# Two edits in a two-layer transformer kernel: where an attention pair's step ends, and where a convolution's last tap is written

## The chip, the cores and the metric

The kernel runs on one core of one Trainium2 chip. The core has four compute engines with a queue each: TensorE (PE, with its weight loads shown as PEld), VectorE (DVE), ScalarE (ACT) and GpSimd (POOL); a fifth, SyncE (SP), issues the DMAs here. Every queue is worked off in order, and an instruction waits on semaphores for what it needs. The metric is the device time of one execution in microseconds, the median of several.

## The reference, cut to what matters

Two layers work on x of 16 sequences, 512 tokens and 256 channels, in float32. In each layer a modulation made from a small conditioning vector scales and shifts a layer norm, and gates what is added back.

- Layer 0 projects to q, k and v, runs a causal convolution of four taps over the tokens of each channel, then Silu; these feed a recurrence of "fast weights" over chunks of 16 tokens, which goes through the tokens in order. A low-rank feed-forward part follows.
- Layer 1 is attention with 16 heads of 16 channels. A token sees the 64 latest tokens and, besides, the first four tokens of its sequence (the global keys). A feed-forward part that mixes each token with the one before it (channel mix) follows.

```
y = lax.conv_general_dilated(xT, w[:, None, :], ..., padding=[(KSZ - 1, 0)], feature_group_count=x.shape[-1])
...
q = l2norm(jax.nn.silu(short_conv(hidden_states @ Wq.T, cq)).reshape(b, l, H, HD))
...
mask = local | g_row & causal | g_col & causal
att = jnp.where(mask, att, jnp.finfo(att.dtype).min)
att = jax.nn.softmax(att, axis=-1)
```

## The kernel before, in words

The work is cut into 16 units: half of the sequences (8) times a block of 64 tokens. A unit u goes through five streams: `prepare` (layer norm, projections and convolutions), `chain` (the recurrence, on DVE, POOL and ACT), `mlp` (end of layer 0's first part and the low-rank feed-forward), `attend` (window attention) and `mix` (channel mix). Each stream is a Python generator, and what lies between two `yield`s is a step. A timetable gives every step a due time in units (`prepare` 12 steps from u - 1.7 to u - 0.7, `chain` 28 steps from u to u + 2, `attend` 24 steps, 19 of them from u + 3.05 to u + 3.95), and the steps of all units are written in the order of these times. So moving a `yield` moves instructions ahead of, or behind, the steps of other streams. From the written order the framework makes the order of each engine's queue; it lets a later instruction go first where an earlier one isn't ready by its plan, and it places buffers and semaphores. The table functions Silu, Gelu and Tanh are issued as bursts (`run`, L220 to L235), the first of a burst waiting for all that the burst needs, so that ACT's table is loaded once for each burst and once back (L224, L234).

Buffers are rings: eight PSUM banks are one for the fast weights (`fw`), three under the tag "bank" (`bank`), four under "abank" (`abank`). SBUF tiles of 2 KB a partition are rings by stream: three for stream a, six for stream c.

Convolution (`prepare`, L434 to L474), for q, k and v (n) and each half of the channels (k2), one step each: PE makes the projection in a bank pp (L441); ACT copies it behind three old columns into xp (L454) and scales the bank by the last weight plus one (L457); DVE adds the other three taps into the same bank (L459). A third step runs the burst of both halves' Silus from the banks to the SBUF tiles y (L465, timed at L224), and SP spills y to DRAM in two pieces each (L468).

Attention works on four pairs of sequences in a unit (r). `find_maxima` (L877) makes the scores sc and their maxima mx (L888), which POOL splits in parts (L215, L217). `weigh` (L904) does the rest of a pair: two filler matmuls (`hold`, L197), a transposition of the maxima (pmx, L908, and mxT, L910), then the scores st again with keys on the partitions, less the maxima (mm, L872), into four banks of "abank"; the mask by a matmul (`add_mask`, L869); the exponentials pT (L926); where the block isn't one of the first two ("far"), also scores tg over the global keys with two fillers, and their exponentials pg (L938); then py (weights times values) and pz (the sums), into two banks of "abank"; then 1/pz as rs (L976, L977) and the product yT (L981). After two pairs, pproj (L1003) projects them, and the gated sum is added to x (up_c, L387, and x, L389).

Other names that the prediction uses: pq and pk are attention's projections (L800, L812); up_a and up_b are the gated sums of layer 0; hp is channel mix's normed input (L367), sg its gate (L1085); e_k and e_v are the recurrence's exponentials (L541), pd_o, pd_i and pd_kv its outer products on POOL (L533), tok its token copies (L596); pgate (L480) is a projection at the end of `prepare`.

Of the kernel before, what the change touches and what calls it, by code (L numbers as in the profile page):

```python
# [12 lines left out]
AF = mybir.ActivationFunctionType  # L13
# [4 lines left out]
P = 128  # L18
# [3 lines left out]
TB = 64  # L22
HB = 8
# [72 lines left out]
def adaln_blocks(ctx: ExitStack, tc: tile.TileContext, a: dict, out: bass.AP):  # L96
    nc = tc.nc
    mul, add, sub = ALU.mult, ALU.add, ALU.subtract
# [12 lines left out]
    def bank(name):  # L111
        return ps.tile([P, 512], F32, tag="bank", name=name)

    def abank(name):
        return ps_a.tile([P, 512], F32, tag="abank", name=name)
# [4 lines left out]
    def t2k(stream, name, shape=None):  # L120
        return work.tile(shape or [P, 512], F32, tag=f"t2k_{stream}", name=name, bufs=RING[stream])
# [23 lines left out]
    conv_w = []  # L145
# [74 lines left out]
    def run(burst, after):  # L220

        with tc.high_priority():
            for k, args in enumerate(burst):
                ins = nc.scalar.activation(*args[0], **args[1])  # L224
                for dep in after if k == 0 else ():
                    tc.add_manual_dep(
                        ins.ins,
                        dep.ins.name,
                        mybir.DependencyInfo(mybir.DependencyClass.Sync, mybir.DependencyReason.DATA),
                        reason="one load of the table",  # L230
                    )
                if k > 0:
                    tc.keep_in_program_order(ins)
            back = nc.scalar.preload_act_table_set("natural_log_exp_and_others")  # L234
            tc.keep_in_program_order(back)  # L235
# [86 lines left out]
    def spill(name, shape):  # L322
        spilled[name] = dram.tile(shape, F32, tag=name, name=name)
        return spilled[name]
# [7 lines left out]
    def hidden(stream, name, cols=TB):  # L332
        t = work.tile([P, 2 * HB * (TB + 1)], F32, tag=f"hT_{stream}", name=name, bufs=1)
        return t[:, : 2 * HB * cols].rearrange("p (k b t) -> p k b t", k=2, b=HB)
# [59 lines left out]
    def place(u):  # L394

        return u % NH, u // NH
# [7 lines left out]
    def load_x(u, name, tag, bufs):  # L404
        x = stage.tile([P, NR, C], F32, tag=tag, name=name, bufs=bufs)
        for e in range(2):
            nc.sync.dma_start(x[e * TB : (e + 1) * TB], rows(a["x"], u, e))
        return x

    def prepare(u):  # L410
        half, tb = place(u)
        b0 = half * HB
        bs = slice(b0, b0 + HB)
        for pc in range(NPC):
            for n in "qkvo":
                spill(f"{n}{u}_{pc}", [HB, H, D, PT])
            spill(f"lr{u}_{pc}", [HB, H, 2, PT])
        x = load_x(u, f"xa{u}", "xa", 1)
        hT = hidden("a", f"hTa{u}")
        yield from norm_T(x, 0, 0, b0, f"a{u}", hT)  # L420
        hf = [hT[:, k].rearrange("p b t -> p (b t)") for k in range(2)]

        pp = bank(f"plr{u}")
        for k in range(2):
            nc.tensor.matmul(pp[: 2 * H, :], lhsT=w_lr[:, k, :], rhs=hf[k], start=k == 0, stop=k == 1)
        lrT = t2k("a", f"lrT{u}", [P, HB, TB])[: 2 * H]
        nc.scalar.copy(lrT.rearrange("p b t -> p (b t)"), pp[: 2 * H, :])
        for pc in range(NPC):
            nc.sync.dma_start(
                spilled[f"lr{u}_{pc}"].rearrange("b h j t -> (h j) b t"),  # L430
                lrT[:, :, pc * PT : (pc + 1) * PT],
            )

        for n in range(3):  # L434
            ys, convs = [], []
            for k2 in range(2):
                tg = tails[:, 2 * n + k2, bs, :]
                tag = f"{u}_{n}_{k2}"
                pp = bank(f"pp{tag}")
                for k in range(2):  # L440
                    nc.tensor.matmul(  # L441
                        pp,
                        lhsT=w_qkv[n][:, k, k2 * P : (k2 + 1) * P],
                        rhs=hf[k],
                        start=k == 0,
                        stop=k == 1,
                    )
                ppb = pp.rearrange("p (b t) -> p b t", b=HB)
                xp = work.tile([P, HB, TB + 3], F32, tag="xp", name=f"xp{tag}", bufs=2)
                if tb == 0:  # L450
                    nc.gpsimd.memset(xp[:, :, 0:3], 0.0)
                else:
                    nc.gpsimd.tensor_copy(xp[:, :, 0:3], tg)
                nc.scalar.copy(xp[:, :, 3:], ppb)  # L454
                if tb < T // TB - 1:
                    nc.gpsimd.tensor_copy(tg, xp[:, :, TB:])
                nc.scalar.activation(ppb, ppb, AF.Copy, scale=conv_w[n][:, k2, 3:4])  # L457
                for j in range(3):
                    ins = nc.vector.scalar_tensor_tensor(  # L459
                        ppb, xp[:, :, j : j + TB], conv_w[n][:, k2, j : j + 1], ppb, mul, add  # L460
                    )
                ys.append((t2k("a", f"y{tag}", [P, HB, TB]), ppb))
                convs.append(ins)
                yield
            run([((y, ppb, AF.Silu), {}) for y, ppb in ys], convs)  # L465
            for k2, (y, _) in enumerate(ys):
                for pc in range(NPC):
                    nc.sync.dma_start(  # L468
                        spilled[f"{'qkv'[n]}{u}_{pc}"][:, k2 * H // 2 : (k2 + 1) * H // 2].rearrange(
                            "b h d t -> (h d) b t"  # L470
                        ),
                        y[:, :, pc * PT : (pc + 1) * PT],
                    )
            yield  # L474

        gT = spill(f"gT{u}", [P, 2, HB * TB])
        for k2 in range(2):
            pp = bank(f"pgate{u}_{k2}")
            for k in range(2):
                nc.tensor.matmul(  # L480
                    pp, lhsT=w_g[:, k, k2 * P : (k2 + 1) * P], rhs=hf[k], start=k == 0, stop=k == 1
                )
            gsb = t2k("a", f"gsb{u}_{k2}")
            nc.scalar.copy(gsb, pp)
            nc.sync.dma_start(gT[:, k2], gsb)
# [283 lines left out]
    def window_attention(i, x):  # L769
# [4 lines left out]
        far, last = tb > 1, tb == T // TB - 1  # L774
# [96 lines left out]
        def mm(dst, lhsT, rhs, start=False):  # L871
            nc.tensor.matmul(dst, lhsT=lhsT, rhs=rhs, start=start, stop=False, skip_group_check=True)  # L872
# [31 lines left out]
        def weigh(r, outs):  # L904
            tag, q = f"{i}_{r}", queries(r)
# [11 lines left out]
            for s, k2, e in slots:  # L917
                for j in range(4):
                    rows = slice(32 * j, 32 * (j + 1))
                    mm(st[j][:, s * P : (s + 1) * P], sel[rows, s : s + 1].to_broadcast([32, P]), mxT[rows])  # L920
            yield
            pT = []
            for j in range(4):
                add_mask(st[j], False)
                pT.append(t2k("c", f"pT{tag}_{j}"))
                nc.scalar.activation(pT[j], st[j], AF.Exp)  # L926
            py, pz = abank(f"py{tag}"), abank(f"pz{tag}")
            if far:

                rg = slice(32 * r, 32 * (r + 1))  # L930
                tg = bank(f"tg{tag}")
                for s, k2, e in slots:
                    mm(tg[rg, e * P : (e + 1) * P], kglob[:, b0 + 2 * r + e, 16 * k2 : 16 * k2 + 32], q(k2, e), s == 0)
                for e in range(2):
                    mm(tg[rg, e * P : (e + 1) * P], selg[:, e], mxT)
                hold(tg[:, 2 * P :], 2)
                pg = work.tile([P, 2 * P], F32, tag="pg", name=f"pg{tag}", bufs=1)
                nc.scalar.activation(pg[rg], tg[rg, : 2 * P], AF.Exp)  # L938
                for s, k2, e in slots:
                    for j in range(4):  # L940
                        cols = slice(k2 * P + 32 * j, k2 * P + 32 * (j + 1))
                        mm(
                            py[32 * j : 32 * (j + 1), s * P : (s + 1) * P],
                            vglob[half][rg, e, cols],
                            pg[rg, e * P : (e + 1) * P],
                            s == 0,
                        )
                for k2 in range(2):
                    for j in range(4):
                        n = 4 * k2 + j  # L950
                        mm(
                            pz[32 * j : 32 * (j + 1), k2 * 2 * P : (k2 + 1) * 2 * P],
                            ones_g[rg, n : n + 1].to_broadcast([32, 32]),
                            pg[rg],
                            k2 == 0,
                        )
# [236 lines left out]
```

## Time and profile before

| | |
|---|---|
| three runs, us | 3237.48, 3243.3 and 3245.96; median 3243.3 |
| profiled execution, us | 3245.84, its span 3244.0 |
| granted TensorE clock, mean | 0.823 |
| PE, DVE, ACT, POOL busy | 75%, 73%, 54%, 52% |
| the convolutions' taps, L459 | 288 of some 750 ns, 215.2 us |
| pT exponentials, L926 | 256 of 619 ns, 133.6 us |
| y Silus, L224 | 96 of 594 ns, 52.1 us |

Busy time of an engine is the union of its instructions; PE's is no measure of how well the array is used. "Idle before" an instruction is the time that its engine stood still ahead of it, with what released it. The chain of waits is followed back from the last instruction, each step to what released it, or to the instruction before it on its engine.

### The profile page before, as it was taken

How to read it: one execution, taken by the hardware profiler on the slowest of the kernel's cores; microseconds unless marked ns; L12 is line 12 of the kernel's file. 1: busy time of each engine (PE TensorE's matmuls, PEld its weight loads, DVE VectorE, ACT ScalarE, POOL GpSimd, SP SyncE). 2: the span in 40 equal slices, each digit the busy share in tenths (PEclk: the TensorE clock that was granted, in tenths of full speed). 3: DMA queues.
4: the chain of work that ended last, by engine and by line, in shares of the span. 5: the costliest groups of instructions: out<-in, count | busy, mean ns of one | idle time of the engine just before them, and what ended most of it. 6: DMA issues, size and time to landing. Idle time of an engine off the chain costs nothing.

```text
span 3244.0 us, 47232 instructions
## 1 busy us (share of the span) xinstructions
PE 2445.9 (75%) x17232; PEld 1472.7 (45%) x17232; DVE 2372.1 (73%) x4513; ACT 1762.4 (54%) x3738; POOL 1677.1 (52%) x1575
## 2 busy tenths in 40 slices
PE   3541156778787778988888888988888888889996
PEld 2110124444444445555455555554545555556564
DVE  1678787878868878878888888878878877873221
ACT  1652354555664656665665656565665545454543
POOL 0245555556656655655646565655556556553112
PEclk8775577878877887988889797989889787879898
DMA  5331112131403223130413122231404121112010
GB/s 150 75 69 20 46 34 70 31 73 39 97 17 77 62 57 76 48 85 21 103 30 94 45 68 65 51 83 34 99 14 105 28 70 37 57 39 59 17 28 27
DMA packets 439307, 186.46 MB, mean 57 GB/s; under 512 B 323937, under 2 KB 413090, under 8 KB 439074
## 3 DMA queue, kind: packets, MB, share of 16 engines
q1 hardware_dynamic: 439074, 183.44, 23.4%
q8 instruction: 135, 2.21, 0.3%
q14 instruction: 98, 0.80, 0.1%
HBM read 116.66 MB, written 66.72 MB: 57 GB/s over the span
## 4 chain that ended last, share of the span: by engine, by line
DVE 35%; POOL 22%; PE 21%; ACT 10%; issue 8%; DMA 3%; SPq 1%; POOLq 0%; DVEq 0%; ACTq 0%
POOL pd_o L533 6%; POOL pd_i L533 5%; DVE pd_kv L630 3%; DVE sc_v L526 3%; DVE pp L459 3%; DVE sv L527 3%; DVE mx L888 2%; DVE do L635 2%; PE st L872 2%; DVE di L635 2%; POOL pd_kv L533 2%; DVE scs L527 2%; PE pQ L742 1%; PE ph L735 1%; PE py L872 1%
## 5 line engine op out<-in xcount | busy, mean ns | idle before, releaser
L533 POOL TENSOR_TENSOR pd_o<-e_k,dt_v 128x1024 f32<-128x1024 f32 x128 | 299.4, 2346 | 242.0 <-DVE e_k L548 242.0
L533 POOL TENSOR_TENSOR pd_i<-e_v,dt_k 128x1024 f32<-128x1024 f32 x128 | 297.3, 2358 | 30.7 <-DVE e_v L548 30.7
L660 POOL TENSOR_TENSOR pd_kv<-hid,pd_kv 128x1024 f32<-128x1024 f32 x64 | 150.5, 2351 | 175.3 <-DVE fw L631 149.3
L872 PE MATMUL st<-qs,keys 32*128 32x128 f32 x2048 | 203.4, 321 | 46.2 <-DVE yT L981 23.3
L635 DVE TENSOR_REDUCE di<-pd_i 128x64 f32<-128x1024 f32 x128 | 155.6, 1216 | 108.6 <-POOL pd_i L533 108.6
L872 PEld LDWEIGHTS st<-qs,keys 32*128 32x128 f32 x2048 | 168.6, 211 | 122.0 <-DVE yT L981 34.3
L872 PE MATMUL sc<-keys,qs 32*128 32x128 f32 x2048 | 167.3, 327 | 74.1 <-DVE yT L981 47.9
L635 DVE TENSOR_REDUCE do<-pd_o 128x64 f32<-128x1024 f32 x126 | 152.9, 1215 | 91.2 <-POOL pd_o L533 91.2
L707 PE MATMUL pwo<-w_WoT,oT 128*128 128x256 f32 x256 | 107.0, 579 | 136.7 <-POOL oT L700 135.9
L872 PEld LDWEIGHTS sc<-keys,qs 32*128 32x128 f32 x2048 | 133.3, 215 | 141.0 <-DVE yT L981 51.2
L888 DVE TENSOR_REDUCE mx<-sc 128x4 f32<-128x512 f32 x256 | 168.0, 682 | 18.5 <-PE sc L869 18.3
L526 DVE TENSOR_TENSOR sc_k<-tok,fw 128x1024 f32<-128x1024 f32 x128 | 155.7, 1216 | 13.8 <-ACT tok L596 12.1
L533 POOL TENSOR_TENSOR pd_kv<-hid,dt_v 128x1024 f32<-128x1024 f32 x64 | 150.5, 2352 | 25.7 <-DVE hid L622 22.7
L630 DVE TENSOR_TENSOR_SCAN pd_kv<-within,pd_kv 128x1024 f32<-128x1024 bf16 x64 | 156.4, 2443 | 0.7
L526 DVE TENSOR_TENSOR sc_v<-tok,fw 128x1024 f32<-128x1024 f32 x128 | 151.0, 1216 | 1.5
L527 DVE TENSOR_REDUCE sv<-sc_v 128x64 f32<-128x1024 f32 x128 | 150.4, 1212 | 0.0
L981 DVE TENSOR_TENSOR yT<-py,rs 128x256 f32<-128x256 f32 x128 | 51.6, 417 | 131.2 <-ACT rs L977 130.8
L735 PE MATMUL ph<-PT,w_v 64*128 64x512 f32 x256 | 119.7, 725 | 34.9 <-ACT z L224 19.8
L707 PEld LDWEIGHTS pwo<-w_WoT,oT 128*128 128x128 f32 x256 | 69.3, 289 | 163.1 <-POOL oT L700 150.3
L1003 PE MATMUL pproj<-w_proj,yT 128*128 128x256 f32 x512 | 129.8, 395 | 17.1 <-DVE yT L981 12.6
L926 ACT ACTIVATE pT<-st 128x512 f32<-128x512 f32 x256 | 133.6, 619 | 15.7 <-PE st L869 15.6
L454 ACT COPY xp<-pp 128x512 f32<-128x512 f32 x96 | 56.6, 589 | 156.8 <-PE pp L441 142.4
(248 smaller groups left out, 7039.2 us busy)
## 6 DMA issues: line engine op xcount, KB each, us to landing
values<-values SPq DMA_DIRECT2D x56, 256.0 KB
gate_a<-gates SPq DMA_DIRECT2D x64, 128.0 KB
xa<-in_x_dram SPq DMA_DIRECT2D x32, 256.0 KB
x<-in_x_dram SPq DMA_DIRECT2D x32, 256.0 KB
gate_c<-gates SPq DMA_DIRECT2D x64, 128.0 KB
gate_d<-gates SPq DMA_DIRECT2D x64, 128.0 KB
q<-y SPq DMA_DIRECT2D x64, 128.0 KB
dt_q<-q SPq DMA_DIRECT2D x32, 256.0 KB
```

Of the source, the lines that this page charges most:

```text
L526: engine.tensor_tensor(pr, tok.unsqueeze(1).to_broadcast(every), w.unsqueeze(2).to_broadcast(every), mul)
L527: nc.vector.tensor_reduce(dst, pr, AX.X, add)
L533: engine.tensor_tensor(pr, hid.unsqueeze(2).to_broadcast(every), tok.unsqueeze(1).to_broadcast(every), mul)
L630: nc.vector.tensor_tensor_scan(flat, within, flat, 0.0, mul, add)
L635: nc.vector.tensor_reduce(t, pr, AX.X, add)
L660: nc.gpsimd.tensor_tensor(po, qh.unsqueeze(2).to_broadcast([P, R, D, CH]), upto, mul)
L707: nc.tensor.matmul(po[:, n * C : (n + 1) * C], lhsT=pair(oT, k, 2 * b2 + n), rhs=w_o[:, k, :], start=k == 0, stop=k == 1,)
L735: nc.tensor.matmul(ph, lhsT=w_v1[rows, f // 2, :], rhs=pT[rows], start=True, stop=True)
L872: nc.tensor.matmul(dst, lhsT=lhsT, rhs=rhs, start=start, stop=False, skip_group_check=True)
L888: nc.vector.tensor_reduce(mx[:, j], sc[j].rearrange("p (s k) -> p s k", s=NS), AX.X, ALU.max)
L926: nc.scalar.activation(pT[j], st[j], AF.Exp)
L1003: nc.tensor.matmul(po[:, n * C : (n + 1) * C], lhsT=yT[:, k2, par].rearrange("p e t -> p (e t)"), rhs=w_proj[:, k2, par, :], start=k2 == 0 ...
```

## The change

Two edits that touch different streams. In the convolution, the tile y is taken before the taps; the third tap writes y in SBUF where it wrote the bank, and Silu works in place on y. In `weigh`, the first `yield` moves down: the masks, the exponentials pT, and for far blocks the scores over the global keys and their exponentials belong now to the step that makes st; the step behind it holds py and pz alone. The number of steps is the same.

```diff
                 nc.scalar.activation(ppb, ppb, AF.Copy, scale=conv_w[n][:, k2, 3:4])
+                y = t2k("a", f"y{tag}", [P, HB, TB])
                 for j in range(3):
                     ins = nc.vector.scalar_tensor_tensor(
-                        ppb, xp[:, :, j : j + TB], conv_w[n][:, k2, j : j + 1], ppb, mul, add
-                    )
-                ys.append((t2k("a", f"y{tag}", [P, HB, TB]), ppb))
+                        y if j == 2 else ppb, xp[:, :, j : j + TB], conv_w[n][:, k2, j : j + 1], ppb, mul, add
+                    )
+                ys.append(y)
                 convs.append(ins)
                 yield
-            run([((y, ppb, AF.Silu), {}) for y, ppb in ys], convs)
-            for k2, (y, _) in enumerate(ys):
+            run([((y, y, AF.Silu), {}) for y in ys], convs)
+            for k2, y in enumerate(ys):
...
                     mm(st[j][:, s * P : (s + 1) * P], sel[rows, s : s + 1].to_broadcast([32, P]), mxT[rows])
-            yield
             pT = []
             for j in range(4):
                 add_mask(st[j], False)
                 pT.append(t2k("c", f"pT{tag}_{j}"))
                 nc.scalar.activation(pT[j], st[j], AF.Exp)
-            py, pz = abank(f"py{tag}"), abank(f"pz{tag}")
             if far:
...
                 nc.scalar.activation(pg[rg], tg[rg, : 2 * P], AF.Exp)
+            yield
+            py, pz = abank(f"py{tag}"), abank(f"pz{tag}")
+            if far:
                 for s, k2, e in slots:
```

## The prediction

> **What bounds the kernel now.** I read the page first, then the windows by stage, the list of waits, and the timeline of one steady period on PE, DVE and ACT.
>
> ```profile
> PE 2445.9 (75%) x17232; PEld 1472.7 (45%) x17232; DVE 2372.1 (73%) x4513; ACT 1762.4 (54%) x3738; POOL 1677.1 (52%) x1575
> DVE 35%; POOL 22%; PE 21%; ACT 10%; issue 8%; DMA 3%; SPq 1%; POOLq 0%; DVEq 0%; ACTq 0%
> ```
> No engine is full. The second line, the chain of waits by engine, passes through all of them, DVE most. The windows (columns: stretch, its length, then busy time of PE, PEld, DVE, ACT, POOL, granted clock, DMA share, GB/s) say where:
>
> ```profile
> 0.00:300.00 300.00, 118.30 (x248) 51.90 (x248) 177.68 (x335) 135.24 (x269) 95.55 (x112) 0.75 0.36 85
> 300.00:900.00 600.00, 362.61 (x1995) 207.96 (x1995) 481.44 (x897) 308.97 (x671) 345.42 (x301) 0.75 0.22 53
> 900.00:2900.00 2000.00, 1665.22 (x12164) 1018.76 (x12162) 1617.88 (x3070) 1163.67 (x2491) 1151.95 (x1048) 0.85 0.24 59
> 2900.00:3244.00 344.00, 299.81 (x2830) 194.08 (x2828) 95.06 (x213) 154.48 (x309) 84.19 (x114) 0.88 0.12 31
> ```
> In the long middle PE is busy 83% and DVE 81%, each waiting for the other; the last 344 us are PE's (87%), with DVE at 28%. The middle is periodic: the same wait of DVE's yT comes at 1691.21, 1872.13 and 2053.05 us, so a unit costs 180.9 us, and what one unit saves is saved some ten times. Inside one unit, PE, then DVE, then ACT:
>
> ```profile
> 1756.39 1.99 PE L1003 MATMUL pproj<-w_proj,yT 128*128 128x256 f32 x8
> 1762.58 3.78 PE L800 MATMUL pq<-hTc,w_w_attnT 128*128 128x512 f32 x4 [4.20 <-ACT y L224]
> ...
> 1769.06 1.03 PE L1003 MATMUL pproj<-w_proj,yT 128*128 128x256 f32 x4
> ```
> ```profile
> 1749.71 0.75 DVE L459 SCALAR_TENSOR_TENSOR pp<-xp,w_ck,pp 128x512 f32<-128x512 f32 x1
> ...
> 1761.14 0.75 DVE L459 SCALAR_TENSOR_TENSOR pp<-xp,w_ck,pp 128x512 f32<-128x512 f32 x1
> ...
> 1771.84 0.69 DVE L387 TENSOR_TENSOR up_c<-pproj,gate_c 128x512 f32<-128x512 f32 x1 [1.99 <-PE pproj L1003]
> ```
> ```profile
> 1761.93 1.08 ACT L224 ACTIVATE y<-pp 128x512 f32<-128x512 f32 x2 [3.48 <-DVE pp L459]
> ```
> This is the place to look at. The convolution of the first half of the channels is done at 1750.46 (1749.71 + 0.75), but its PSUM bank stays taken until its Silu at 1761.93 has read it, because the Silus of both halves run as one burst behind both convolutions. PE, free since 1758.38, stands still for 4.20 us with the attention's projection pq, which wants one of the three "bank" banks; DVE then waits 1.99 us for pproj, which stands behind pq and pk.
>
> **The change part by part.**
>
> *The last tap to SBUF.* Three things change. (1) 96 third taps on DVE read PSUM and write SBUF. The tap takes 750 ns now (L459); the nearest row with PSUM in and SBUF out is L1085, sg, the same operation and size, 675 ns. 96 x 0.075 = 7.2 us of DVE; L459 has 3% of the span on the chain, 97 of its 215 us, so 45% of that counts: -3 us. The bounds are 0 and -7. (2) 96 Silus on ACT read SBUF. The pair of rows for it is L976 (rs out of PSUM, 594 ns) and L977 (out of SBUF, 640 ns): +46 ns each, 4.4 us of ACT, which has 10% of the chain: +0.4 us. [...] (3) The bank is free after the third tap, not after the Silu. PE's waits for "ACT y" add up to 108 us (pp 48.2, pgate 25.8, pq 33.5, pk 0.9). Middle: from 1042 us on seven units lose 4.2 to 6.3 us before pq, two others about 1. PE has some 27 us of idle time in a unit (153.8 busy of 180.9), and later in it waits 3.7 us for DVE's up_a and 5.5 us for DVE's yT, so PE alone gives its 4.2 us back. What stays is what DVE gets: 1.99 us at up_c. With the two short ones as one, 8 x 2.0 = -16 us. Bounds: 0, if DVE gives that back at its waits for POOL (7.3 us a unit for pd_i), and -33, all of PE's waits before pq. Start: ten waits before 264 us, PE busy 39%; the chain passes through two of them, each worth the 2 to 3 us between tap and Silu: -5 us. Conv edits: -3 + 0.4 - 16 - 5 = -24 us.
>
> A wait is added: the third tap now needs the y buffer (ring of three), so on DVE it may stand for the spill of y three buffers back, with the recurrence behind it. In the unit shown, the Silu of the step before is at 1732.96 and the tap that takes that buffer at 1761.14: 28 us of cover. At the start a spill issued from 89.20 was landed when its reload was issued at 93.00, under 4 us. Priced at zero; without that cover it would be some 2 us per unit. The DMAs stay as many, behind the same Silu on SP's queue.
>
> *The pair's step.* No instruction is added. Mask matmuls (4), exponentials (4 x 619 ns), the tg matmuls with their two fillers, and the pg exponential (371 ns) belong now to the step before; py and pz keep theirs. Nothing of it issues a DMA or runs on POOL, so SP's and POOL's queues are passed by nothing. A step of attention is 0.9/19 of a unit, 8.6 us of priority. Gain: PE waits 38.7 us for pg and 30.2 us for pT over the kernel. If other work is slipped in there, the 69 us are filled, but in the middle PE's idle time is given back as above, and in the tail, where PE leads, there is little to slip in (10.2 of the 38.7 us lie there). I take 10%: -7 us, bounds 0 and -40. Loss: per pair 2.85 us of ACT go up to 8.6 us ahead. What can be late next are the recurrence's e_k and e_v exponentials (259 and 313 ns), which DVE and then POOL wait for. In the unit shown all four pairs start their exponentials within 2.6 us of their masks already; the widest but one:
>
> ```profile
> 1813.79 1.03 PE L869 MATMUL st<-masks,ident_bf 128*128 128x512 bf16 x4
> ...
> 1813.99 2.48 ACT L367 ACTIVATE hp<-pt_d,mod 128x64 f32<-128x64 f32 x8 [1.83 <-PE pt_d L361]
> ...
> 1816.32 2.10 ACT L926 ACTIVATE pT<-st 128x512 f32<-128x512 f32 x4
> ...
> 1818.64 1.08 PE L872 MATMUL py<-pg,vglob 32*32 32x128 f32 x32 [1.66 <-ACT pg L938]
> ```
> and what is overtaken is then hp, not the recurrence. I take three overtakings of 2.85 us among the 48 pairs of the middle's twelve units, since this unit shows none: +8 us; bounds 0 and +137 (every pair). Steps together +1 us. The pT buffers (ring of six) are also wanted earlier, beside two yT held for pproj; the pproj that frees them is two steps earlier: zero, and a wait for it would fall under the loss above.
>
> The sum: -24 + 1 = -23 us. The profiled execution took 3245.84 us (span 3244.0), 2.5 us over the median 3243.3 of three runs, so 3222.8 against it and 3220 against the median.
>
> **The rivals.** A difference under 0.3%, 9.7 us, is no change here.
>
> A, likeliest (0.50): the bank is free earlier, DVE loses its wait at up_c, the step matters little: -12 to -42, 3220.
>
> B, given back (0.13): PE reaches up_a and yT earlier and waits there; DVE gives its 2 us to pd_i. What remains are the taps, -3, and the noise of a new order: about 3240. For it speak POOL's pd_i and pd_o, DVE's longest waits (108.6 and 91.2 us); against it that the chain runs through y, pq, pk, pproj and up_c.
>
> C, slower (0.25): the exponentials go ahead of the recurrence on ACT. Place: ACT's queue, ahead of e_k, e_v and the tok copies; price 2.85 us for each pair that does it. It decides from 24/2.85, some 9 of the 64 pairs, on. Two pairs a unit over 12 units would be 24 x 2.85 = +68, less the 24: about 3287; with half of those 3253. For it: POOL's pd_o waits 242.0 us for DVE's e_k, so the recurrence has no slack there. Against it: ACT waits 136.9 us for DVE before e_k, and so is often free when it comes.
>
> D, more (0.08): PE's waits for y and for pg and pT are all filled and DVE follows: -33 - 20 - 8, about 3182.
>
> E, the added wait (0.04): the y ring makes DVE stand, or the earlier tg bank takes from the convolutions what they gave: some 2 us for each of 16 units, 3243 + 32 - 24, and more at the start: 3255.
>
> **How the numbers follow.** Faster: A and D, 0.58. Same: B, 0.13. Slower: C and E, 0.29. The range leaves out the end of D and the far end of C: 3170 to 3282. A alone: 3201 to 3231.
>
> **What would show it.** The third tap near 675 ns and y near 640; no wait of PE for ACT y, pq starting right behind pproj; up_c's wait for pproj smaller; a unit of 178 to 179 us in place of 180.9; PE's waits for pg and pT below half of 69 us. I am wrong if the unit is as long as before although pq no longer waits (B), or if it is longer with ACT's e_k or tok directly behind pT exponentials and DVE or POOL waiting for them (C).

## The result, and the profile after

The changed kernel takes 3235.2 us against 3245.2 (medians of 20 runs each, taken side by side): a ratio of 0.9967, with a 95% interval from 0.9956 to 0.9978. That is 10 us faster, between a third and a half of the 23 us forecast. The profiled execution has a span of 3229.5 us, 14.5 less than before.

The page's busy times, after:

```profile
PE 2385.4 (74%) x17232; PEld 1452.9 (45%) x17232; DVE 2395.3 (74%) x4513; ACT 1783.6 (55%) x3748; POOL 1673.0 (52%) x1575
```

The windows by stage, after (columns as before):

```profile
0.00:300.00 300.00, 113.19 (x248) 49.47 (x248) 182.57 (x340) 136.38 (x270) 95.76 (x112) 0.70 0.36 85
300.00:900.00 600.00, 361.48 (x2083) 211.62 (x2083) 484.05 (x910) 311.19 (x675) 349.03 (x304) 0.75 0.22 53
900.00:2900.00 2000.00, 1624.59 (x12067) 1003.04 (x12070) 1628.65 (x3048) 1180.22 (x2495) 1144.18 (x1045) 0.84 0.24 59
2900.00:3230.00 330.00, 286.16 (x2844) 188.81 (x2837) 100.01 (x217) 155.80 (x309) 84.06 (x114) 0.92 0.12 32
```

The busy times do not show the gain: PE has 60 us less than before, DVE 23 us more, ACT 21 us more. DVE's growth surprises, since its taps should have become shorter. Of ACT's 21 us, 12.8 are ten more loads of its table (232 of 1283 ns, 222 before) that no edit wrote: the table is not loaded just once for each burst and once back, and how often depends on the queues' order (f6 below, with both edits in another order, has 222 again).

At the place that the forecast was about, the timeline of PE after shows what was expected:

```profile
1759.62 3.62 PE L1005 MATMUL pproj<-w_proj,yT 128*128 128x256 f32 x16
1763.08 1.88 PE L801 MATMUL pq<-hTc,w_w_attnT 128*128 128x512 f32 x4
```

pq stands right behind pproj, with no wait for a Silu. PE's waits for "ACT y", 108 us before, are gone from the list; waits for the third tap, shorter, stand in their place, and those for pg and pT are as they were (38.7 and 30.2 us before):

```profile
PE py L873 <- ACT pg L937: 36.6, 15, 5.3
PE py L873 <- ACT pT L926: 30.0, 11, 5.3
PE pp L441 <- DVE y L460: 19.0, 7, 6.1
PE pgate L481 <- DVE y L460: 11.5, 2, 7.1
PE pq L801 <- DVE y L460: 9.1, 4, 6.6
```

Yet the unit did not become shorter. The recurrence has four scans a unit on DVE (pd_kv from `within`; L630 before, L631 after), so nine scans in a row span two units. The scans of one stretch, with their shortest, median and longest time in ns, and the start of the first and the last; before, then after:

```profile
L630 DVE TENSOR_TENSOR_SCAN pd_kv<-within,pd_kv x9: 2272/2275/2292, 1722.7 to 2084.6; 128x1024 f32<-128x1024 bf16 x9
```
```profile
L631 DVE TENSOR_TENSOR_SCAN pd_kv<-within,pd_kv x9: 2275/3022/4371, 1725.8 to 2090.9; 128x1024 f32<-128x1024 bf16 x9
```

Before, 361.9 us for two units, 180.9 each; after, 365.1, 182.6 each. By the first scan of each unit, the changed kernel is 4.4 us ahead at unit 1 (310.9 against 315.3), 19.1 ahead at unit 6 (1164.5 against 1183.6), level at unit 15 (2803.1 against 2802.7), and wins 15 us behind it. A second trace of the changed kernel (b2_after, below) is 15.1 us ahead at unit 6, 4.2 us behind at unit 15, and wins 17.7 us behind it, so two traces of one kernel can lie some 4 us apart. In both, the gain lies at the start and in the tail, and the middle, where the forecast put it, gave 19 us back.

### The profile page after: what moved, and what is told of

It reads as the page before. It is cut to its first block, busy times and chain, and to the rows that moved or that the text cites. A ratio compares the mean times of both kernels' runs of the same rounds, so it can differ in the third digit from the quotient of the medians.

```text
span 3229.5 us, 47324 instructions
## 1 busy us (share of the span) xinstructions
PE 2385.4 (74%) x17232; PEld 1452.9 (45%) x17232; DVE 2395.3 (74%) x4513; ACT 1783.6 (55%) x3748; POOL 1673.0 (52%) x1575
## 4 chain that ended last, share of the span: by engine, by line
DVE 33%; PE 22%; POOL 20%; ACT 12%; issue 8%; DMA 4%; SPq 1%; POOLq 0%; DVEq 0%; ACTq 0%
POOL pd_o L534 5%; POOL pd_i L534 4%; DVE pd_kv L631 4%; DVE sc_v L527 3%; POOL pd_kv L534 3%; DVE sv L528 3%; DVE do L636 2%; PE st L873 2%; DVE di L636 2%; DVE sc_k L527 2%; DVE pp L460 2%; PE pproj L1005 2%; DMA oT<-o 2%; DVE scs L528 2%; DVE mx L889 1%
## 5 line engine op out<-in xcount | busy, mean ns | idle before, releaser
L534 POOL TENSOR_TENSOR pd_o<-e_k,dt_v 128x1024 f32<-128x1024 f32 x128 | 301.0, 2358 | 171.4 <-DVE e_k L549 171.3
L873 PE MATMUL st<-qs,keys 32*128 32x128 f32 x2048 | 191.3, 336 | 71.7 <-DVE yT L983 29.0
L873 PE MATMUL sc<-keys,qs 32*128 32x128 f32 x2048 | 183.1, 326 | 71.7 <-DVE mx L889 41.7
L873 PEld LDWEIGHTS st<-qs,keys 32*128 32x128 f32 x2048 | 160.5, 226 | 132.2 <-DVE mx L889 32.4
L873 PEld LDWEIGHTS sc<-keys,qs 32*128 32x128 f32 x2048 | 148.0, 216 | 141.9 <-DVE mx L889 58.8
L631 DVE TENSOR_TENSOR_SCAN pd_kv<-within,pd_kv 128x1024 f32<-128x1024 bf16 x64 | 174.4, 2725 | 0.9
L224 ACT ACT_TABLE_LOAD x111 | 142.4, 1283 | 14.3 <-PE ph L736 7.6
L736 PE MATMUL ph<-PT,w_v 64*128 64x512 f32 x256 | 111.1, 669 | 38.0 <-ACT z L224 27.8
L1005 PE MATMUL pproj<-w_proj,yT 128*128 128x256 f32 x512 | 122.9, 386 | 11.2 <-DVE yT L983 9.3
L197 PE MATMUL pmx<-w_w_attnT,blocks 128*128 128x384 f32 x256 | 118.5, 593 | 13.4 <-ACT hp L367 9.4
```

The costliest lines, as they stand in the source:

```text
L534: engine.tensor_tensor(pr, hid.unsqueeze(2).to_broadcast(every), tok.unsqueeze(1).to_broadcast(every), mul)
L631: nc.vector.tensor_tensor_scan(flat, within, flat, 0.0, mul, add)
L1005: nc.tensor.matmul(po[:, n * C : (n + 1) * C], lhsT=yT[:, k2, par].rearrange("p e t -> p (e t)"), rhs=w_proj[:, k2, par, :], start=k2 == 0 ...
```

## The experiments

The changed kernel's queues stand in another order than those before, on every engine (2743 of DVE's 4513 places hold an instruction that writes another tile): the framework makes each queue's order by its own plan of what is ready when, and both edits change that plan. Below, such an order is called a deal, and a kernel whose queues the framework orders again is dealt anew. So the runs had to tell two things apart, what an edit does in a given order, and what the new order does. Ratios are to the kernel before, run beside each.

**The two edits apart, and two variants.** e1_conv has the convolution edit alone; e2_weigh the step's edit alone. e3_hold is e1 with a small reader that keeps the bank; e4_pT_only is the changed kernel with tg and pg left behind the `yield`:

```diff
# e3_hold, behind the burst of Silus, for both halves
+                late = work.tile([P, 1], F32, tag="late", name=f"late{u}_{n}_{k2}", bufs=2)
+                nc.scalar.activation(late, ppb[:, 0, :1], AF.Copy, scale=y[:, 0, :1])
# e4_pT_only, in weigh
                 nc.scalar.activation(pT[j], st[j], AF.Exp)
+            yield
+            py, pz = abank(f"py{tag}"), abank(f"pz{tag}")
             if far:
...
                 nc.scalar.activation(pg[rg], tg[rg, : 2 * P], AF.Exp)
-            yield
-            py, pz = abank(f"py{tag}"), abank(f"pz{tag}")
-            if far:
```

Expected of e1_conv: 

> The convolution edit alone. Theory G (the step's edit gives back): the convolution edit is worth its forecast -24 us, so this kernel stands at about 3221 against 3245, some 13 us below the changed kernel. Theory M (the convolution edit was priced too high): it is worth the measured -10 us by itself, 3235, and the step's edit is worth nothing. Theory S (the step's edit is what pays): -2 to 0 us here, 3243 to 3245. Theory N (every edit deals the queues anew, and the differences are those of the new orders): the parts do not add up to the whole, in any direction, by up to some 15 us.

Expected of e2_weigh: 

> The step's edit alone (exponentials, tg and pg ahead of the first yield). Theory G: +10 to +15 us, 3255 to 3260, with ACT's pT waiting for PE's st (73 us in the changed kernel, 16 us before). Theory M: 3245, within 3 us. Theory S: about 3235. Theory N: a difference that together with the convolution edit's does not make -10.

Expected of e3_hold: 

> The convolution edit alone, with the bank held as long as before: a scalar operation of one element per partition that reads the bank and the finished y stands behind the two Silus (96 small operations on ACT, estimated at 0.2 to 0.25 us each, some 20 us of ACT's 1760, of which ACT's 10% on the chain counts 2 us). If the earlier release of the bank is what the convolution edit gives, this kernel is back at 3245 plus 0 to 4 us, PE's waits before pq come back to some 4 us a unit (released by ACT late), and the start, too, is as before. If the taps in SBUF are what it gives, it keeps the gain of the convolution edit alone, less 2 us.

Expected of e4_pT_only: 

> The changed kernel with only the masks and the four pT exponentials ahead of the first yield; tg, its two fillers and the pg exponential stay behind it. Theory G with the tg bank as the culprit (tg takes one of the three bank banks a step earlier and keeps it while its exponential queues): about 3221, all of the convolution edit's gain. Theory G with the pT exponentials as the culprit (ACT stands ahead of them): as the changed kernel, 3235, ACT's pT wait for st still above 50 us. Theory M: 3235. Theory N: off both by up to 15 us.

| | us | ratio, 95% interval |
|---|---|---|
| e1_conv | 3347.8 | 1.0320 (1.0305 to 1.0334) |
| e2_weigh | 3337.6 | 1.0287 (1.0272 to 1.0303) |
| e3_hold | 3386.7 | 1.0436 (1.0418 to 1.0453) |
| e4_pT_only | 3254.6 | 1.0032 (1.0019 to 1.0045) |

Alone, one edit costs 103 us and the other 93; together they win 10. Theory N was the only one that allowed for parts that don't add up, and even it was too tame. The loss is periodic. The scans of two units of e1_conv:

```profile
L631 DVE TENSOR_TENSOR_SCAN pd_kv<-within,pd_kv x9: 2268/3946/4151, 1729.4 to 2125.4; 128x1024 f32<-128x1024 bf16 x9
```

That is 198 us a unit, with the same instructions as in the other kernels, loads of ACT's table aside. e3_hold answers nothing about the bank, since it was dealt anew as well, and for the same reason e4's 19 us over the changed kernel say nothing about tg and pg.

The granted clock is a rival for this loss: over these two units it is 0.81 in e1, where it was 0.87, and PE is busy 322.5 us, where it was 307.7. But e2, with the same 198 us a unit, has PE busy 311.4 us, at 0.83. So a longer busy PE is not needed for such a loss; what part of e1's it makes is not shown.

**The order held.** The next kernels pin every queue. Behind the last written instruction, each instruction gets an issue-order edge, without a semaphore, to the one that stood ahead of it in the queue of another kernel:

```diff
+    put_in_order(tc)
...
+        for a, b in zip(places, places[1:]):
+            tc.add_manual_dep(
+                queue[b],
+                queue[a].name,
+                mybir.DependencyInfo(mybir.DependencyClass.NoSync, mybir.DependencyReason.DATA),
```

f1_conv_in_before is e1 in the order of before; f6_after_in_e2 the changed kernel in e2's order; f7_hold_in_before is e3 in the order of before. n1_later holds nothing, and is the kernel before with a timetable that is off by next to nothing:

```diff
-        yield attend, [(2, u + 2.65, u + 2.8), (3, u + 2.95, u + 3.05), (19, u + 3.05, u + 3.95)]
+        yield attend, [(2, u + 2.65, u + 2.8), (3, u + 2.95, u + 3.05), (19, u + 3.06, u + 3.96)]
```

Expected of f1_conv_in_before: 

> The convolution edit alone, with every engine's queue held in the order that the kernel before has (an issue-order edge from each instruction to the next on its engine; nothing else is added). Theory O (the two edits alone are slow because the scheduler deals the queues anew; in a given order the convolution edit is worth what was forecast, less the taps): 3222 to 3235, unit of 179 to 180 us, no wait of PE for the Silu. Theory W (in that order PE's wait is given back elsewhere): 3243 to 3247, unit of 180.9 us. Theory T (the edit itself costs, whatever the order): above 3300, as the convolution edit alone.

Expected of f6_after_in_e2: 

> The changed kernel with every queue held in the order that the step's edit alone got (3338 us). Theory O: the order carries the time, so it stays near 3338, less what the convolution edit is worth in a given order (0 to 24 us): 3314 to 3338, and nowhere near 3235. If the edits themselves carried the time it would be 3235.

Expected of f7_hold_in_before: 

> As the convolution edit alone in the order of before, with the bank held by a scalar operation of one element per partition on the bank and the finished y (96 of them, in ACT's queue right behind the two Silus and the table load). If the bank's earlier release is all of what the edit gives in a given order: 3245 plus 0 to 5 us, PE's waits before pq back at 4 us or more a unit. If taps and Silus on SBUF carry part of it, it stands below 3245 by that part.

Expected of n1_later: 

> The kernel before with the attention's nineteen steps placed 0.01 of a unit later in the timetable (1.8 us by its own due times); no instruction, buffer or dependency differs. It asks how far a new deal of the queues alone moves the time. Theory O: by tens of us, in the middle's period (a unit well off 180.9 us). Theory T (the time follows from what the edits do): 3245 within 5 us.

| | us | ratio, 95% interval |
|---|---|---|
| f1_conv_in_before | 3239.7 | 0.9987 (0.9980 to 0.9995) |
| f6_after_in_e2 | 3336.1 | 1.0282 (1.0266 to 1.0298) |
| f7_hold_in_before | 3285.3 | 1.0115 (1.0091 to 1.0139) |
| n1_later | 3283.3 | 1.0122 (1.0103 to 1.0141) |

The order carries the time. In e2's order the kernel with both edits is as slow as e2 (3336.1 and 3337.6). In the order of before the convolution edit is worth 1.6 to 6.5 us, not the loss of 103 it shows when dealt anew, and in e2's order its worth can't be told from nothing. What the edges cost by themselves was not tried; a kernel held in its own order would show it. And a shift of 0.01 unit, which edits nothing, costs 39 us. Theory O holds for the order; for the size, f1 lies between O (3222 to 3235) and W (3243 to 3247), and its unit is no shorter (181.2 us), as W has it.

f1 is the clean test of the forecast: the traces of f1 and before show the same tile written at every place of every engine's queue (the third tap's aside), and only the banks' release, the taps and the Silus changed. PE and then DVE, in the unit that the prediction showed:

```profile
1751.71 1.99 PE L1004 MATMUL pproj<-w_proj,yT 128*128 128x256 f32 x8
1753.54 1.88 PE L801 MATMUL pq<-hTc,w_w_attnT 128*128 128x512 f32 x4
1757.35 3.42 PE L813 MATMUL pk<-hTc,w_w_attnT 128*128 128x512 f32 x4 [1.94 <-DVE e_k L541]
1762.14 1.13 PE L1004 MATMUL pproj<-w_proj,yT 128*128 128x256 f32 x4 [1.36 <-DVE yT L982]
```
```profile
1756.46 0.74 DVE L460 SCALAR_TENSOR_TENSOR y<-xp,w_ck,pp 128x512 f32<-128x512 f32 x1
...
1765.07 0.67 DVE L387 TENSOR_TENSOR up_c<-pproj,gate_c 128x512 f32<-128x512 f32 x1
1768.32 0.75 DVE L347 BATCH_NORM_STATS2 st_d<-x 128x6 f32<-128x256 f32 x2 [2.38 <-POOL x L389]
```

The 4.20 us before pq are gone. PE gives 3.30 of them back within nine us: pk starts 0.15 us after the second half's third tap has ended (1756.46 + 0.74 = 1757.20), so it most likely waits for that bank (the profile puts the wait down to e_k, which ended later), and pproj waits for DVE's yT. DVE's up_c no longer waits, and comes 2.1 us earlier, counted from the unit's first scan (47.1 us behind it, 49.1 before). But st_d, the next layer norm's first step, reads x from POOL, and waits 2.38 us where it waited 1.20 before:

```profile
1773.92 0.75 DVE L347 BATCH_NORM_STATS2 st_d<-x 128x6 f32<-128x256 f32 x2 [1.20 <-POOL x L389]
```

POOL's queue shows why, before and then f1:

```profile
1769.37 2.35 POOL L533 TENSOR_TENSOR pd_o<-e_k,dt_v 128x1024 f32<-128x1024 f32 x1 [7.14 <-DVE e_k L548]
1772.61 1.27 POOL L389 TENSOR_TENSOR x<-x,up_c 128x512 f32<-128x512 f32 x1 [0.89 <-DVE up_c L387]
```
```profile
1764.69 2.35 POOL L534 TENSOR_TENSOR pd_o<-e_k,dt_v 128x1024 f32<-128x1024 f32 x1 [7.15 <-DVE e_k L549]
1767.00 1.28 POOL L389 TENSOR_TENSOR x<-x,up_c 128x512 f32<-128x512 f32 x1
```

Before, POOL was done with the recurrence's pd_o and waited 0.89 us for up_c. In f1, up_c is there at 1765.74 (1765.07 + 0.67), but x stands behind pd_o in POOL's queue, and pd_o starts when the recurrence's e_k comes. So of the 2.1 us, 1.2 are gone at st_d; the rest of them goes at later waits of DVE. Over six units, before and then f1, the two waits are:

```profile
DVE up_c L387 <- PE pproj L1003: 10.6, 6, 2.1
DVE st_d L347 <- POOL x L389: 7.5, 6, 1.6
```
```profile
DVE st_d L347 <- POOL x L389: 13.2, 6, 2.4
DVE up_c L387 <- PE pproj L1004: 1.5, 1, 1.5
```

With two other layer norms that read x, DVE's waits for POOL's x grow by 8.0 us (10.8 to 18.8), close to the 9.0 that the waits for pproj lose; those for pd_i stay (45.2 and 45.6). The windows of the same six units, before and f1:

```profile
1541.70:2635.30 1093.60, 923.83 (x6911) 563.09 (x6913) 888.38 (x1692) 657.61 (x1392) 628.35 (x584) 0.86 0.27 63
```
```profile
1536.30:2631.50 1095.20, 925.30 (x6906) 563.63 (x6909) 887.35 (x1691) 658.30 (x1392) 627.30 (x584) 0.86 0.27 63
```

PE's idle time is 1093.60 - 923.83 = 169.8 us before, and 169.9 in f1; DVE's 205.2, and 207.9. Nothing of the 4.20 us, or of the 1.99, stays in the middle. f1's lead is 3.3 us at unit 1 (312.0 against 315.3), 5.4 at unit 8 (1536.3 against 1541.7) and 1.0 at unit 15; 4.5 us more come in the tail behind it, where PE is busy 371.3 us in place of 375.8. With one trace of each kernel, and a scatter of some 4 us between traces, it is not shown where the 4.4 us by which f1's median is lower arise.

f7's time missed both its expectations, though PE's wait before pq did come back (36.8 us for the reader, 33.5 for the Silu before). The reader stands behind the table load of 1.28 us that follows the Silus, so that the bank was held longer than before, and its 96 instructions of 258 ns keep ACT busy for some 25 us. It shows that a bank released later can cost where one released earlier brings nothing, but not which of the two costs made the 45 us over f1.

**How far a deal scatters, and whose queue it is.** n2 and n3 put the shift of n1 on the changed kernel and on e1. s1 and s2 hold one queue of e1 in the order of before (PE's, or DVE's), and leave the other four to be dealt around it, by one more line in the edit above:

```diff
+        if name not in ("EngineType.PE",):
+            continue
```

Expected of n2_after_later: 

> The changed kernel with the same 0.01 of a unit on the attention's steps that cost the kernel before 39 us. Theory L (its 10 us are one draw of a deal that scatters by tens of us, with at most 4 of them the convolution edit's own): anywhere from 3235 to 3350, most likely 10 us or more above the changed kernel. Theory E (the two edits together give the queues an order that is good for a reason of theirs): within 5 us of 3235.

Expected of n3_conv_later: 

> The convolution edit alone (3348 us) with the same 0.01 of a unit. Theory L: its 103 us were the deal, so this one falls elsewhere, by 20 us or more from 3348, most likely below it, since 3348 is the worst but one seen. Theory E: the convolution edit alone is bad for a reason of its own and stays within 10 us of 3348.

Expected of s1_pe_held: 

> The convolution edit alone, with PE's queue alone held in the order that the kernel before has; the other four queues are dealt again by the scheduler around it. If PE's order is what makes the unit of the convolution edit alone 198 us in place of 181, this stands near 3240 (unit about 181). If it is the order on DVE, ACT and POOL, it stays above 3320.

Expected of s2_dve_held: 

> The same with DVE's queue alone held in the order of before. If DVE's order carries the 17 us a unit: near 3240, unit about 181 us. If PE's order does: above 3320. If neither alone, both this and the one with PE's queue held stand between, 3260 to 3320.

| | us | ratio, 95% interval |
|---|---|---|
| n2_after_later | 3301.0 | 1.0178 (1.0155 to 1.0201) |
| n3_conv_later | 3288.9 | 1.0132 (1.0108 to 1.0156) |
| s1_pe_held | 3361.6 | 1.0362 (1.0339 to 1.0386) |
| s2_dve_held | 3261.0 | 1.0053 (1.0036 to 1.0071) |

The same shift costs the changed kernel 66 us and gives e1 59 back. So the 10 us won are of one deal, as the 103 us lost are; Theory L holds. PE's old order alone cures nothing: with it held, e1 is as slow as free. With DVE's held, the time is 3261.0, still 20 us over the kernel before, but the unit is 182.6 us (365.2 for two) and the scans are as short as before:

```profile
L631 DVE TENSOR_TENSOR_SCAN pd_kv<-within,pd_kv x9: 2269/2276/2292, 1735.6 to 2100.8; 128x1024 f32<-128x1024 bf16 x9
```

This does not set DVE's queue apart from the others: with it held, they fall nearly into the old order too. ACT's queue writes another tile than before in 624 of its 3738 places, where e1's does so in 2484.

**The start and the middle exchanged.** h6 is e1's program, in the changed kernel's order up to the recurrence's first instruction of unit 6, from there in that of before; g2 is the changed kernel the other way round. s4 puts e1's DVE queue into the kernel before, s3 holds ACT's queue of e1 in the order of before.

Expected of h6_after_start: 

> The convolution edit with every queue held: up to the first chunk of unit 6 in the order of the changed kernel, from there in the order of the kernel before. If the changed kernel's lead of 19 us at unit 6 is its order's (15 us of it beyond the convolution edit in the order of before), the lead is kept with the old order of the middle: 3240 - 15 = 3225, and this beats both kernels by 10 to 20 us. If the lead is given back at the seam, because units 6 to 15 are bound to the same pace wherever they start: 3235 to 3240.

Expected of g2_before_start: 

> The changed kernel with every queue held: up to the first chunk of unit 6 in the order of before, from there in its own. If the lead at the start is the order's and the middle of the changed kernel (182.6 us a unit) is its order's too: 3235 + 15 = 3250, slower than before. If the start's lead comes from what the edits do (the bank, the taps) it stays near 3235 to 3238.

Expected of s4_dve_of_conv: 

> The kernel before with DVE's queue alone held in the order that the convolution edit alone got (3348 us), the other four queues dealt again around it. If DVE's order carries the loss of the convolution edit alone: above 3310, unit 193 us or more. If it needs the other queues' orders too: 3245 to 3300.

Expected of s3_act_held: 

> The convolution edit alone with ACT's queue alone held in the order of before. DVE's queue held alone gave 3261. If it is DVE's order and nothing else: above 3320 here. If any queue through which the recurrence runs pins the others (ACT holds e_k, e_v and the tok copies): 3240 to 3270, as with DVE's.

| | us | ratio, 95% interval |
|---|---|---|
| h6_after_start | 3234.8 | 0.9970 (0.9959 to 0.9981) |
| g2_before_start | 3247.6 | 1.0013 (1.0004 to 1.0021) |
| s4_dve_of_conv | 3416.3 | 1.0532 (1.0516 to 1.0547) |
| s3_act_held | 3226.6 | 0.9942 (0.9924 to 0.9961) |

With the old order at its start the changed kernel loses 12 us and all of its gain. h6 got less than the 3225 expected, and close to the number of the other answer, but not for its reason: it is at 1172.2 us at unit 6, since the seam costs 5 us of the lead (its unit 5 takes 180.7 us, the changed kernel's 175.7; the rest of the difference is no more than the scatter between traces), but the 8 us that it has on f1 there (1179.9) it still has at the end (spans 3230.5 and 3238.5; the medians differ by 4.9). So a lead from the start is carried through. s4 shows DVE's order from the other side: with taps still in PSUM it makes the kernel before slower than e1 itself, and there, too, the others follow (ACT's queue differs from e1's in 298 places). With ACT's order held, DVE's differs from before in 608 places, where e1's does in 2939, and the re-deal lands well, so DVE's queue is not the only one that pins the others.

**A rival version.** s3 seemed to beat the change; both once more, on one chip:

Expected of b1_act_held: 

> The convolution edit alone with ACT's queue held in the order of before, once more and beside the changed kernel on the same chip: 3227 again (ratio 0.992 to 0.996 to the kernel before), below the changed kernel. If 3227 was luck of one chip: 3235 or above.

Expected of b2_after: 

> The changed kernel as it is, for comparison on the same chip: 3235, ratio 0.9956 to 0.9978 to the kernel before.

b1_act_held took 3233.2 us (0.9968, 0.9956 to 0.9981), b2_after 3232.2 us (0.9959, 0.9946 to 0.9972). They are equal: no version that beats both kernels was found. But the convolution edit, with ACT's old order held, does without the step's edit what the two do together.

## Why the prediction was right or wrong

**Two steps failed.** One is the largest term of the sum, "what DVE gets: 1.99 us at up_c", -16 us: in the order of before, in which the prediction read it, it is 0. The other is a term that the sum puts at nothing without a reason: "the noise of a new order" is a word in rival B, and n1, n2 and n3 measure +39, +66 and -59 us for an edit of nothing. The measured -10 us lies between A (-12 at least) and B (about 3240), and none of the rivals held the cause. That the direction came out right is luck: of the eight kernels that were wholly dealt anew (the changed one, e1 to e4, n1 to n3) it alone is faster than before.

**"What stays is what DVE gets: 1.99 us at up_c", 8 x 2.0 = -16 us.** In the held order it is 0. The mechanism up to pq and up_c was right; the next link was wrong. DVE, freed 2 us earlier, waits for POOL's x: that is rival B's course, which had 0.13, though B put the wait at pd_i. In the changed kernel's own order the middle is longer by 1.7 us a unit.

**Start, -5 us.** 3.3 us at unit 1 and some 4 to 5 at units 6 to 8 in the held order: the size forecast. But only 1.0 is left at unit 15, so that it counts at the end is not shown. (The waits for the Silu before 264 us are eleven, not ten; the sum does not use the count.) In the changed kernel the lead at unit 6 is 15 to 19 us, and the rest of it is the order's: that is what g2 takes away.

**Third tap 675 ns, -3 us.** It takes 739 to 743 ns, against 747 to 751 for the taps that write the bank. The lines by shape, after:

```profile
L460 DVE SCALAR_TENSOR_TENSOR pp<-xp,w_ck,pp x64: 725/747/756, 87.6 to 2493.6; 128x512 f32<-128x512 f32 x64
...
L460 DVE SCALAR_TENSOR_TENSOR y<-xp,w_ck,pp x32: 729/743/749, 89.7 to 2494.4; 128x512 f32<-128x512 f32 x32
```

96 x 7 ns is 0.7 us of DVE in place of 7.2. The row of sg has the same operation and size, but it takes a constant where the tap takes a factor for each partition from SBUF, and its SBUF input is not a window of eight rows as xp's is. Whether either of these makes the difference of some 65 ns was not tried.

**Silu +46 ns.** 595 before, 624 after:

```profile
L224 ACT ACTIVATE y<-y x96: 613/624/634, 89.8 to 2530.4; 128x512 f32<-128x512 f32 x96
```

+29 ns each, 2.8 us of ACT: right in sign, and smaller than the 46 ns of the rows of rs.

**The step, +1 us.** PE's waits for pg and pT were to fall below half of 69 us; they stayed at 66.6. What C saw did come: ACT stands ahead of its pT exponentials, before and after:

```profile
ACT pT L926 <- PE st L869: 15.6, 15, 2.6
```
```profile
ACT pT L926 <- PE st L870: 73.4, 51, 4.3
```

But C's price did not: POOL's wait of pd_o for e_k fell from 242.0 to 171.3 us. Since the step's edit is nothing but a change of order, its worth can't be told apart from the deal.

**The sum in the held order**: taps -0.3, Silu +0.3, middle 0, start -3 to -5 if it lasts, in all -3 to -5, where f1 measured -1.6 to -6.5. By subtraction, the other 6 us of the change's 10 are the deal's: a start better by some 11 to 15 us, scans longer by 18 us of DVE (below), and a tail 15 us shorter, where the granted clock is 0.92 and was 0.88. From unit 15 on, PE is busy 362.2 us in place of 375.8, which is nearly the whole of the tail's gain, with nearly the same number of matmuls and a clock of 0.88 in place of 0.85. The kernels in the changed kernel's order there have the same (g2: 361.4 us), those in the order of before do not (h6: 371.3 us at 0.86). Why the clock is granted higher was not found.

**What stays open.** Which neighbours in DVE's queue make a unit of 198 us was not found. Of e1's 17 us a unit, DVE's busy time holds 6.3 (309.15 us over two units against 296.58); the rest are waits over all engines. The convolution edit's worth in the changed kernel's own order wasn't tried: there PE's queue has the banks' next users ahead of work that the Silus need, and taps left in PSUM would probably close a circle of waits.

## What to carry to other kernels

Where a scheduler deals the queues, price an edit with every queue held in its old order, and put beside it an edit of nothing (a due time moved by a hundredth of a unit) to see how far a new deal scatters; a gain below that scatter can be the deal's, and be lost with the next edit. A wait that is removed from one engine is worth only what the next two links of the loop don't wait for: follow the freed engine to its next wait, and the engine behind it as well. A row of the same operation and size need not price another: here the inputs also differed, and 675 ns became 739 to 743.

## What the runs showed of the hardware

The scan on DVE is stretched by POOL, in the changed kernel from 2.28 us to as much as 4.41. Two scans of the changed kernel on DVE, and what POOL did meanwhile:

```profile
1725.75 4.37 DVE L631 TENSOR_TENSOR_SCAN pd_kv<-within,pd_kv 128x1024 f32<-128x1024 bf16 x1
1736.97 3.02 DVE L631 TENSOR_TENSOR_SCAN pd_kv<-within,pd_kv 128x1024 f32<-128x1024 bf16 x1
```
```profile
1725.62 2.35 POOL L534 TENSOR_TENSOR pd_kv<-hid,dt_v 128x1024 f32<-128x1024 f32 x1 [1.46 <-DVE hid L623]
...
1736.59 1.26 POOL L675 TENSOR_TENSOR dt_q<-dt_q,om 128x512 f32<-128x512 f32 x1 [1.58 <-ACT om L674]
```

POOL's product ends at 1725.62 + 2.35 = 1727.97, and the scan 2.15 us later; dt_q ends at 1737.85, and the second scan 2.14 us later. A scan of this kernel beside an idle POOL takes 2.28. In all 23 stretched scans of the changed kernel the scan ends 2.14 to 2.15 us after the POOL operation that was running at its start. So, by these times, such a scan stands until that one is done, and then runs. Two short operations of POOL did not stretch the scan that started beside them: a memset, which reads nothing (0.95 us; the scan took 2.28 in the changed kernel), and rs_c, a power of 4 columns read from SBUF (1.04 us; 2.27 to 2.29 in s3 and b1).

Counted over the traces, 9 of the 64 scans are above 2.5 us before and in f1, f7, s2 and h6, 15 in s3 and b1, and 21 to 28 in the others, the changed kernel (23) and e1 (22) among them. So the stretching does not explain e1's loss. The scans' mean goes from 2443 to 2725 ns with the change: 64 x 0.282 = 18 us of DVE that no edit wrote, and how many a kernel gets goes with its order.
